# A mixture-of-experts router: the four experts from one Max of eight and a replacement, its tokens a part sooner, its steps dealt denser

## The chip, the cores and the metric

The kernel runs on one core of one Trainium2 chip. A core has five engines with a queue each, taken in order: TensorE (PE in the profile, its weight loads PEld), VectorE (DVE), ScalarE (ACT), GpSimd (POOL) and SyncE (SP, which only starts transfers here). They meet through semaphores. The metric is the device time of one execution in microseconds (us).

## The reference

A transformer block on x of 4 x 512 tokens with 512 features: layer norm, cross attention of 16 heads against a context of 1601 rows (257 image rows and 1344 text rows, a softmax for each kind), a residual sum, layer norm again, and a feed-forward part with a shared network and 32 routed experts. All is float32. What bears on the change is the router, over all 2048 tokens (T), and what the experts do with it:

```python
scores = jax.nn.sigmoid(x @ router_w.T)                     # T x 32
sc = scores + e_bias[None, :]
gs = sc.reshape(T, NG, E // NG)                             # 8 groups of 4 experts
group_scores = lax.top_k(gs, 2)[0].sum(-1)
_, gidx = lax.top_k(group_scores, TKG)                      # 3 groups stay
...
masked = jnp.where(smask > 0, sc, 0.0)
_, topk_idx = lax.top_k(masked, K)                          # 4 experts
topk_w = jnp.take_along_axis(scores, topk_idx, axis=1)
topk_w = topk_w / (topk_w.sum(-1, keepdims=True) + 1e-20) * SCALE
```

Each expert takes the first C = 80 tokens that chose it, in the order of the tokens. Its output for them, silu(x W_gate) * (x W_up) W_down, is scaled by the weight and added to the token's row, beside the shared network's output and the residual.

## The kernel before

The kernel is one long program whose order is written by hand; nothing reschedules it. It goes over the four batches b. For each it makes keys and values of the context (sixteen key parts: four blocks of context by four chunks of features), then the attention, four heads at a time, over 13 key tiles; the output projection, the second layer norm and the router product of batch b (`residual`) run inside the next batch's key parts, and for the last batch inside the tail.

**Routing** (`routing`, called with a batch) returns two lists of small steps for its 512 tokens, laid out as 128 partitions by four token groups (t) by 32 experts. The first list, `work`: the sigmoid on ScalarE (or exponential, sum and reciprocal), the bias, the best two of each group by pairs of maxima and minima, the groups' ranks by comparing all pairs, the mask of the three best groups (`cand`), and then a loop over the four experts that takes for each the maximum, marks where it is, breaks ties to the lowest index by means of `rev` (32, 31, ... 1), adds the mark to `chosen` and pushes the candidate down by 3e38. Then the weights, their DMA into `xw_d` (rows of normed x followed by the 32 weights), and `ranks`: TensorE transposes `chosen` to experts by tokens (four 128x128 transposes, L614), and VectorE makes keys of it in which an earlier token is larger. The second list, `search`: ten Max operations and nine MatchReplace over 80 + 512 keys, which keep each expert's first 80 tokens (`best`) over all batches so far.

The lists of batches 0 and 1 are mixed into the attention loop (two steps a key tile in the last chunk of heads, then seven steps a key part of the next batch). Those of batches 2 and 3 come in the **tail**, `first` and `second`. There the shared network is cut into 32 parts (`units[0]`: gate, up and down products of 8 matmul passes, about 3.43 us each on TensorE), numbered i. A small dealer, `deal(i)`, runs after each part: it spends an account, `SHARE` for each part gone by, 0.3 for a small step and 0.8 for a step of the search, and takes from `first`, then from `second`. `second` is made at part `ready` = 16, since the last batch's router products end with part 15; there `deal(16)` is called ahead of the part itself.

Two parts before the last the kernel empties both lists, and `tokens()` turns `best` into token numbers: two VectorE operations (`past`), a transpose on TensorE (L930), a copy to integers (`tok`). Then six gathers (GpSimd's indirect DMAs, L1003) fetch the tokens of the first six experts out of `xw_d`. The experts follow, one after the other: transposes of the gathered rows (`turn`), `gate_up`, `down`, and a scatter that adds into the output. Their weights, 1.5 MB each, are fetched up to six experts ahead on SyncE's queue, the first of them during the tail's parts (one expert each fourth part).

Of the kernel before, what the change touches and what calls it, by code (L numbers as in the profile page):

```python
# [9 lines left out]
F32 = mybir.dt.float32  # L10
# [3 lines left out]
ALU = mybir.AluOpType  # L14
AX = mybir.AxisListType
# [3 lines left out]
P = 128  # L19
# [7 lines left out]
NQ = L // P  # L27
T = B * L
NT = T // P
E, I, TOPK, NG, TKG = 32, 256, 4, 8, 3  # L30
# [5 lines left out]
BIG = 3.0e38  # L36
# [73 lines left out]
def body(ctx, tc, a, ident, mhalf, logits, x1_d, xw_d, xnT_d, den_d, rec_d, out):  # L110

    nc = tc.nc
# [12 lines left out]
    def psum(dt=F32):  # L125

        shape = [P, 512] if dt is F32 else [P, NQ, P]
        banks.append(banks.pop(0))
        return ring.tile(shape, dt, name="ps", tag=f"bank{banks[-1]}")
# [364 lines left out]

    rt = pool("rt", 1)
    e_b = rt.tile([P, E], F32, name="e_b")
    rev = rt.tile([P, 1, E], F32, name="rev")
    below = rt.tile([P, NG, NG], F32, name="below")

    merged = rt.tile([E, CAP + L], F32, name="merged")  # L500
# [1 line left out]

    def routing_constants():
        nc.scalar.dma_start(e_b, a["e_bias"].partition_broadcast(P))
        nc.gpsimd.iota(rev[:, 0, :], [[-1, E]], base=E, channel_multiplier=0, allow_small_or_imprecise_dtypes=True)
        nc.gpsimd.memset(below, 1.0)

        nc.gpsimd.affine_select(below, below, [[1, NG], [-1, NG]], ALU.is_gt, 0.0, base=0, channel_multiplier=0)
        nc.vector.memset(best, 0.0)

    def routing(b, space, by_exp=False):


        tt, ts, tr = nc.vector.tensor_tensor, nc.vector.tensor_scalar, nc.vector.tensor_reduce
        lo = b * NQ
        taken = []

        def carve(*shape):

            n = NQ  # L520
            for d in shape:
                n *= d
            at = sum(taken)
            taken.append(n)
            names = " ".join("abc"[:len(shape)])
            return space[:, at:at + n].rearrange(
                f"p (t {names}) -> p t {names}", t=NQ, **dict(zip("abc", shape))
            )

        lg = logits[:, lo:lo + NQ, :]  # L530

        both = carve(4 * E)
        first_half, second_half = space[:, :2 * NQ * E], space[:, 2 * NQ * E:4 * NQ * E]
        gt, eq = (x.rearrange("p (t a b) -> p t a b", t=NQ, a=NG) for x in (first_half, second_half))
        cand, hit, sel, chosen = (
            space[:, k * NQ * E:(k + 1) * NQ * E].rearrange("p (t e) -> p t e", t=NQ) for k in range(4)
        )
        sc, sb = carve(E), carve(E)
        m = [carve(NG) for _ in range(4)]
        gs, rank, top = carve(NG), carve(NG), carve(1)  # L540
        g = sb.rearrange("p t (g k) -> p t g k", k=EG)
        one = gs.unsqueeze(3).to_broadcast([P, NQ, NG, NG])
        oth = gs.unsqueeze(2).to_broadcast([P, NQ, NG, NG])
        rv = rev.to_broadcast([P, NQ, E])
        before = below.unsqueeze(1).to_broadcast([P, NQ, NG, NG])

        def wide_(x):
            return x.to_broadcast([P, NQ, E])

        if by_exp:  # L550

            work = [
                lambda: nc.scalar.activation(sc, lg, AF.Exp, scale=-1.0),
                lambda: ts(sc, sc, 1.0, None, ALU.add),
                lambda: nc.vector.reciprocal(sc, sc),
            ]
        else:
            work = [lambda: nc.scalar.activation(sc, lg, AF.Sigmoid)]
        work += [
            lambda: tt(sb, sc, e_b.unsqueeze(1).to_broadcast([P, NQ, E]), ALU.add),  # L560

            lambda: tt(m[0], g[:, :, :, 0], g[:, :, :, 1], ALU.max),
            lambda: tt(m[1], g[:, :, :, 0], g[:, :, :, 1], ALU.min),
            lambda: tt(m[2], g[:, :, :, 2], g[:, :, :, 3], ALU.max),
            lambda: tt(m[3], g[:, :, :, 2], g[:, :, :, 3], ALU.min),
            lambda: tt(m[1], m[1], m[3], ALU.max),
            lambda: tt(m[3], m[0], m[2], ALU.min),
            lambda: tt(m[0], m[0], m[2], ALU.max),
            lambda: tt(m[1], m[1], m[3], ALU.max),
            lambda: tt(gs, m[0], m[1], ALU.add),  # L570

            lambda: tt(gt, oth, one, ALU.is_gt),
            lambda: tt(eq, oth, one, ALU.is_equal),
            lambda: tt(eq, eq, before, ALU.mult),
            lambda: tt(gt, gt, eq, ALU.add),
            lambda: tr(rank, gt, AX.X, ALU.add),
            lambda: ts(rank, rank, float(TKG), None, ALU.is_lt),
            lambda: tt(
                cand.rearrange("p t (g k) -> p t g k", k=EG), g, rank.unsqueeze(3).to_broadcast([P, NQ, NG, EG]), ALU.mult
            ),  # L580
        ]

        for k in range(TOPK):
            into = sel if k else chosen
            work += [
                lambda: tr(top[:, :, 0], cand, AX.X, ALU.max),
                lambda: tt(hit, cand, wide_(top), ALU.is_equal),
                lambda: tt(hit, hit, rv, ALU.mult),
                lambda: tr(top[:, :, 0], hit, AX.X, ALU.max),
                lambda into=into: tt(into, hit, wide_(top), ALU.is_equal),  # L590
            ]
            if k:
                work.append(lambda: tt(chosen, chosen, sel, ALU.add))
            if k < TOPK - 1:
                work.append(
                    lambda into=into: nc.vector.scalar_tensor_tensor(cand, into, -BIG, cand, ALU.mult, ALU.add)
                )
        work += [
            lambda: tt(sb, chosen, sc, ALU.mult),
            lambda: tr(top[:, :, 0], sb, AX.X, ALU.add),  # L600
            lambda: ts(top, top, 1e-20, None, ALU.add),
            lambda: nc.vector.reciprocal(top, top),
            lambda: ts(top, top, SCALE_ROUTE, None, ALU.mult),
            lambda: tt(sb, sb, wide_(top), ALU.mult),
            lambda: nc.sync.dma_start(
                xw_d[lo * P:(lo + NQ) * P, D:].rearrange("(t p) e -> p t e", p=P), sb
            ),
        ]
        key = merged[:, CAP:]

        def ranks():
            ps = psum()
            for i in range(NQ):
                nc.tensor.transpose(ps[:E, i * P:(i + 1) * P], chosen[:, i, :], ident)  # L614
            nc.vector.scalar_tensor_tensor(key, ps[:E, :], float(T), key, ALU.mult, ALU.add)

        work += [
            lambda: nc.gpsimd.iota(
                key, [[-1, L]], base=T - b * L, channel_multiplier=0, allow_small_or_imprecise_dtypes=True
            ),  # L620
            lambda: nc.vector.tensor_copy(merged[:, :CAP], best),
            ranks,
        ]
        search = []
        for j in range(CAP // 8):
            at = best[:, 8 * j:8 * j + 8]
            search.append(lambda at=at: nc.vector.max(at, merged))
            if j < CAP // 8 - 1:
                search.append(lambda at=at: nc.vector.match_replace(merged, at, merged, 0.0))
        return work, search  # L630
# [5 lines left out]
    qT, sq_q, turn, work = queries(0, first_x, L)  # L636
# [281 lines left out]
            nc.sync.dma_start(t, a[name][e])  # L918
            weights.setdefault(e, []).append(t)

    SHARE = 2.4
    AHEAD, WEIGHTS = 6, 6

    def tokens():

        past = ew.tile([E, CAP], F32, name="past", bufs=1)
        nc.vector.tensor_scalar(past, best, T + 0.5, float(T), ALU.is_gt, ALU.mult)
        nc.vector.scalar_tensor_tensor(past, past, float(T), best, ALU.add, ALU.subtract)
        ps = psum()
        nc.tensor.transpose(ps[:CAP, :E], past, ident[:E, :E])  # L930
        nc.vector.tensor_copy(tok, ps[:CAP, :E])
# [149 lines left out]
    for i, u in enumerate(units):  # L1081
        if i < 2:
            continue
        if i == len(units) - 2:
            for f in first + second:
                f()
            first, second = [], []
            tokens()
            for e in range(AHEAD):
                gather(e)  # L1090
        if i == ready:

            space = mid.tile([P, 2, L], F32, name="rb")
            second = sum(routing(B - 1, space.rearrange("p k t -> p (k t)")), [])
            deal(i)
        u()
        for f in side.get(i, ()):
            f()
        later.step()
        deal(i)  # L1100
        if i % 4 == 0 and i // 4 - 1 < WEIGHTS:
            expert_weights(i // 4 - 1)
# [57 lines left out]
```

## Time and profile before

| | |
|---|---|
| three runs | 1705.07, 1705.36, 1710.23 us; median 1705.36 |
| profiled execution | 1705.17 us, its span 1703.5 |
| TensorE | 1681.4 us busy, mean granted clock 0.998 |
| VectorE | 974.6 us busy, 2016 instructions |
| tail: shared parts of units[0] | from about 1327 to 1461 us |
| tail: experts and what is left of the shared network | about 1461 to 1695 us |
| VectorE busy, 1340 to 1400 | 44.6 of 60 us |
| VectorE busy, 1400 to 1460 | 37.9 of 60 us |
| VectorE busy, 1500 to 1600 | 12.9 of 100 us |

Times inside the profile count from the span's start, and a line number (L614) is one of the kernel before. A timeline line gives start, duration, engine, line, operation, what it writes and reads, how many instructions it merges, and in brackets the time that the engine stood idle before it and what it waited for. A matmul's end is modelled, so two consecutive ones overlap a little in the listing; the distance between starts is the better measure. A row of windows gives, for a stretch, its length, then for each engine the busy time and the number of instructions, then the granted clock of TensorE (1.00 is full), the busy share of the DMA engines and GB/s.

### The profile page before, as it was taken

Reading aid. Unit: us, or ns where it says so; the run is one execution under the profiler, and the core shown is the slowest. Engines: PE = TensorE matmul, PEld = TensorE weight load, DVE = VectorE, ACT = ScalarE, POOL = GpSimd, SP = SyncE. Lnnn points to the kernel's source line nnn. Section 1 sums busy time; section 2 is a strip of 40 time slices with the busy share of each in tenths; the row PEclk is TensorE's granted clock in tenths of the full one; section 3 lists DMA queues with packets and bytes.
Section 4 is the critical chain, followed back from the end, with each engine's and each line's share of the span. In section 5 each row is a group of like instructions: output and inputs, shape, how many; then the busy total and the mean of one; then the engine's idle time right before and its main releaser. Section 6 shows DMA issues by size and latency. Waiting matters only on the chain. (4 is left out here: it accounts for less than half of the span.)

```text
span 1703.5 us, 29448 instructions
## 1 busy us (share of the span) xinstructions
PE 1681.4 (99%) x11753; PEld 881.8 (52%) x11753; DVE 974.6 (57%) x2016; ACT 647.3 (38%) x1378; POOL 874.1 (51%) x622
## 2 busy tenths in 40 slices
PE   8999999999999999999999999999999999999997
PEld 4564444456544444565444445654443354677773
DVE  4765555757655549776665597766656767111110
ACT  2135456611354565114545651145557310111111
POOL 3237977332569764426698543276884210233332
PEclk9999999999999999999999999999999999999999
DMA  7000100321100103120000040210002365699964
GB/s 233 1 2 1 27 27 2 114 67 62 38 1 28 27 2 129 51 79 22 2 26 27 2 165 21 75 44 2 14 15 84 112 212 187 199 291 290 296 162 62
DMA packets 67817, 136.30 MB, mean 80 GB/s; under 512 B 16096, under 2 KB 28512, under 8 KB 65632
## 3 DMA queue, kind: packets, MB, share of 16 engines
q1 hardware_dynamic: 60400, 119.91, 21.1%
q0 software_dynamic: 6272, 12.92, 4.1%
q8 instruction: 93, 1.52, 0.4%
q10 hardware_dynamic: 1008, 1.59, 0.3%
q14 instruction: 44, 0.36, 0.1%
HBM read 111.58 MB, written 22.81 MB: 79 GB/s over the span
## 5 line engine op out<-in xcount | busy, mean ns | idle before, releaser
L372 ACT ACTIVATE pT<-ps 128x512 f32<-128x512 f32 (+1 forms) x832 | 429.5, 604 | 346.2 <-PE ps L371 335.7
L334 DVE TENSOR_REDUCE mx<-ps 128x1 f32<-128x512 f32 (+1 forms) x576 | 330.9, 616 | 265.3 <-PE ps L320 265.3
L387 POOL TENSOR_TENSOR acc<-acc,pT 128x1024 f32<-128x1024 f32 x192 | 445.6, 2357 | 3.0 <-ACT pT L372 2.6
L379 PE MATMUL po<-pT,v 128*32 128x512 f32 (+2 forms) x1792 | 222.3, 603 | 0.0
L290 PEld LDWEIGHTS ps<-v_w,cT 128*128 128x128 f32 (+1 forms) x1408 | 169.0, 186 | 102.2 <-DVE mx L334 56.1
L371 PE MATMUL ps<-qT,kT 32*128 32x512 f32 (+1 forms) x1664 | 213.8, 587 | 0.0
L320 PE MATMUL ps<-kT,qT 32*128 32x512 f32 (+1 forms) x1536 | 206.4, 549 | 0.0
L290 PE MATMUL ps<-v_w,cT 128*128 128x128 f32 (+1 forms) x1408 | 197.7, 285 | 0.0
L231 PE MATMUL ps<-cT,wk 128*128 128x512 f32 (+1 forms) x384 | 156.3, 552 | 6.1 <-DMA wk<-in_k_w 6.1
L308 DVE TENSOR_REDUCE mx<-ps 128x1 f32<-128x512 f32 (+2 forms) x256 | 128.1, 562 | 6.4 <-PE ps L305 6.4
L1038 POOL DMA_INDIRECT out<-y,tok x32 | 45.4, 1420 | 133.7 <-DMA out<-y,tok 72.8
L231 PEld LDWEIGHTS ps<-cT,wk 128*128 128x128 f32 x384 | 70.5, 193 | 77.6 <-issue 56.9
L368 PEld LDWEIGHTS <-pick 32*128 32x128 bf16 (+1 forms) x832 | 21.7, 92 | 165.7 <-issue 164.0
L238 POOL TENSOR_TENSOR sq_k<-sq_k,sq 128x512 f32<-128x512 f32 (+2 forms) x48 | 49.5, 1031 | 108.3 <-ACT sq L235 108.0
L298 ACT COPY v<-ps 128x128 f32<-128x128 f32 (+1 forms) x208 | 60.1, 289 | 117.7 <-PE ps L290 117.3
L1028 DVE TENSOR_TENSOR ehT<-ehT,ps 128x160 f32<-128x160 f32 x32 | 10.3, 321 | 158.3 <-ACT ehT L1027 139.1
L394 POOL TENSOR_TENSOR acc<-pT 128x1024 f32<-128x1024 f32 x24 | 56.1, 2359 | 86.9 <-ACT pT L372 54.3
L387 POOL TENSOR_TENSOR pT<-pT 65x1024 f32<-65x1024 f32 x24 | 56.0, 2350 | 87.1 <-PE po L379 78.2
L320 PEld LDWEIGHTS ps<-kT,qT 32*128 32x128 f32 x1536 | 82.1, 183 | 31.0 <-issue 10.1
L387 DVE TENSOR_TENSOR acc<-acc,pT 128x1024 f32<-128x1024 f32 (+1 forms) x72 | 96.7, 1390 | 2.1 <-ACT pT L372 2.1
L379 PEld LDWEIGHTS po<-pT,v 128*32 128x32 f32 (+2 forms) x1792 | 35.0, 107 | 118.6 <-issue 109.3
L368 PE MATMUL ps<-mT,pick 32*128 32x512 bf16 (+1 forms) x832 | 82.6, 386 | 2.4 <-ACT mT L359 2.4
(243 smaller groups left out, 2189.4 us busy)
## 6 DMA issues: line engine op xcount, KB each, us to landing
W_gate<-in_W_gate SPq DMA_DIRECT2D x32, 512.0 KB
W_up<-in_W_up SPq DMA_DIRECT2D x32, 512.0 KB
W_down<-in_W_down SPq DMA_DIRECT2D x32, 512.0 KB
rb<-rec_d SPq DMA_DIRECT2D x64, 128.0 KB
xt<-in_x SPq DMA_DIRECT2D x30, 256.0 KB
cT<-in_ctxT SPq DMA_DIRECT2D x7, 1024.0 KB
wki<-in_k_img_w SPq DMA_DIRECT2D x4, 1024.0 KB
wo<-in_o_w SPq DMA_DIRECT2D x4, 1024.0 KB
```

The lines of the kernel that those rows point to most:

```text
L231: nc.tensor.matmul(ps[:, :n], lhsT=wt[:, k, c * P:(c + 1) * P], rhs=xT[:, k, to], start=k == 0, stop=k == NC - 1)
L290: nc.tensor.matmul(ps[lo:hi, :], lhsT=cTs[bl][:, k, at:at + hi - lo], rhs=ws[bl == NB - 1][:, k, c * P:(c + 1) * P], start=k == 0, stop=k ...
L298: nc.scalar.copy(v[:n, t, :], ps[:n])
L308: nc.vector.tensor_reduce(mx[:, qt, g, bl:bl + 1], ps[:, :n], AX.X, ALU.max, negate=True)
L320: nc.tensor.matmul(ps[:, j * n:(j + 1) * n], lhsT=qT[r:r + HD, c, q * P:(q + 1) * P], rhs=kT[r:r + HD, c, k0:k0 + n], start=True, stop=True,)
L334: nc.vector.tensor_reduce(mx[:, qt, g, i:i + 1], ps[:, :m], AX.X, ALU.max, negate=True)
L368: nc.tensor.matmul(ps[:n], lhsT=pick[r:r + HD, kind(t), :n], rhs=mT[r:r + HD, :], start=True, stop=False)
L371: nc.tensor.matmul(ps[:n], lhsT=kT[r:r + HD, c, t * P:t * P + n], rhs=qT[r:r + HD, c, :], start=False, stop=True)
L372: nc.scalar.activation(pT[:n, g, :], ps[:n], AF.Exp)
L379: nc.tensor.matmul(po[r:r + HD, :], lhsT=v[rows, t, r:r + HD], rhs=pT[rows, g, :], start=start, stop=stop)
L387: (nc.vector if idle else nc.gpsimd).tensor_tensor(to[rows, h, :], to[rows, h, :], pT[rows, h, :], ALU.add)
L394: (nc.vector if idle else nc.gpsimd).tensor_tensor(acc[:, h, :], pTs[0][:, h, :], pTs[1][:, h, :], ALU.add)
```

## The change

Three edits go together.

**The selection.** The loop over four experts and the constant `rev` go. In their place: `cand` becomes the first 32 columns of rows of 36 (`filled`), whose last four hold −1.5e38; for each of the four token groups one Max gives the eight largest of the 32; the last four of these are overwritten by −1.5e38; for each group one MatchReplace writes −3e38 over the first place that holds each of those eight values, so that the four largest are struck out of the candidates, and the other four values find the filling; `chosen` is where the candidate is greater than what is left.

**The tokens.** `tokens` is split: the two VectorE operations (`kept_tokens`) and the emptying of the lists come three parts before the end instead of two; the transpose, the copy and the gathers stay where they were.

**The dealing.** `SHARE` goes from 2.4 to 2.7.

```diff
-        cand, hit, sel, chosen = (
-            space[:, k * NQ * E:(k + 1) * NQ * E].rearrange("p (t e) -> p t e", t=NQ) for k in range(4)
+
+        row_ = E + 8 - TOPK
+        filled, rest_ = (
+            space[:, k * NQ * row_:(k + 1) * NQ * row_].rearrange("p (t e) -> p t e", t=NQ) for k in range(2)
         )
+        cand = filled[:, :, :E]
+        chosen = space[:, 2 * NQ * row_:2 * NQ * row_ + NQ * E].rearrange("p (t e) -> p t e", t=NQ)
...
+            lambda: nc.vector.memset(filled[:, :, E:], -BIG / 2),
             lambda: tt(
                 cand.rearrange("p t (g k) -> p t g k", k=EG), g, rank.unsqueeze(3).to_broadcast([P, NQ, NG, EG]), ALU.mult
             ),
         ]
-        for k in range(TOPK):
-            into = sel if k else chosen
-            work += [
-                lambda: tr(top[:, :, 0], cand, AX.X, ALU.max),
-                lambda: tt(hit, cand, wide_(top), ALU.is_equal),
-                lambda: tt(hit, hit, rv, ALU.mult),
-                lambda: tr(top[:, :, 0], hit, AX.X, ALU.max),
-                lambda into=into: tt(into, hit, wide_(top), ALU.is_equal),
-            ]
-            if k:
-                work.append(lambda: tt(chosen, chosen, sel, ALU.add))
-            if k < TOPK - 1:
-                work.append(
-                    lambda into=into: nc.vector.scalar_tensor_tensor(cand, into, -BIG, cand, ALU.mult, ALU.add)
-                )
+        work += [lambda t=t: nc.vector.max(largest8[:, t, :], cand[:, t, :]) for t in range(NQ)]
+        work += [lambda: nc.vector.memset(largest8[:, :, TOPK:], -BIG / 2)]
+        work += [
+            lambda t=t: nc.vector.match_replace(rest_[:, t, :], largest8[:, t, :], filled[:, t, :], -BIG)
+            for t in range(NQ)
+        ]
+        work += [lambda: tt(chosen, cand, rest_[:, :, :E], ALU.is_gt)]
...
-    SHARE = 2.4
+    SHARE = 2.7
...
-    def tokens():
+    def kept_tokens():
         past = ew.tile([E, CAP], F32, name="past", bufs=1)
         nc.vector.tensor_scalar(past, best, T + 0.5, float(T), ALU.is_gt, ALU.mult)
         nc.vector.scalar_tensor_tensor(past, past, float(T), best, ALU.add, ALU.subtract)
+        return past
+
+    def tokens(past):
         ps = psum()
...
-        if i == len(units) - 2:
+        if i == len(units) - 3:
             for f in first + second:
                 f()
             first, second = [], []
-            tokens()
+            past = kept_tokens()
+        if i == len(units) - 2:
+            tokens(past)
             for e in range(AHEAD):
                 gather(e)
```

More of the change, by code (lines that the diff above doesn't have):

```diff
@@ L496, in body @@
     e_b = rt.tile([P, E], F32, name="e_b")
-    rev = rt.tile([P, 1, E], F32, name="rev")
     below = rt.tile([P, NG, NG], F32, name="below")
@@ L504, in routing_constants @@
         nc.scalar.dma_start(e_b, a["e_bias"].partition_broadcast(P))
-        nc.gpsimd.iota(rev[:, 0, :], [[-1, E]], base=E, channel_multiplier=0, allow_small_or_imprecise_dtypes=True)
         nc.gpsimd.memset(below, 1.0)
@@ L534, in routing @@
         gt, eq = (x.rearrange("p (t a b) -> p t a b", t=NQ, a=NG) for x in (first_half, second_half))
-        cand, hit, sel, chosen = (
-            space[:, k * NQ * E:(k + 1) * NQ * E].rearrange("p (t e) -> p t e", t=NQ) for k in range(4)
-        )
+        row_ = E + 8 - TOPK
+        filled, rest_ = (
+            space[:, k * NQ * row_:(k + 1) * NQ * row_].rearrange("p (t e) -> p t e", t=NQ) for k in range(2)
+        )
+        cand = filled[:, :, :E]
+        chosen = space[:, 2 * NQ * row_:2 * NQ * row_ + NQ * E].rearrange("p (t e) -> p t e", t=NQ)
         sc, sb = carve(E), carve(E)
         m = [carve(NG) for _ in range(4)]
-        gs, rank, top = carve(NG), carve(NG), carve(1)
+        gs, rank, top, largest8 = carve(NG), carve(NG), carve(1), carve(8)
         g = sb.rearrange("p t (g k) -> p t g k", k=EG)
@@ L543, in routing @@
         oth = gs.unsqueeze(2).to_broadcast([P, NQ, NG, NG])
-        rv = rev.to_broadcast([P, NQ, E])
         before = below.unsqueeze(1).to_broadcast([P, NQ, NG, NG])
```

## The prediction

> **What bounds the kernel now.** I read the page's busy table first, then the list of what TensorE waited for over the whole span, then the order of time around the two places that the change moves.
>
> ```profile
> PE 1681.4 (99%) x11753; PEld 881.8 (52%) x11753; DVE 974.6 (57%) x2016; ACT 647.3 (38%) x1378; POOL 874.1 (51%) x622
> ...
> PE ps L231 <- DMA wk<-in_k_w: 6.1, 1, 6.1
> ...
> PE ps L930 <- DVE past L928: 1.2, 1, 1.2
> PE ps L225 <- DVE xpT L1016: 0.7, 1, 0.7
> PE ps L614 <- DVE v L593: 0.7, 2, 0.3
> ```
>
> The first line is the page's, the others are from the list of TensorE's waits (total, times, longest). TensorE is busy 99% of the span and waits 12.9 us in all in that list, 6.1 of them for the first weights. So VectorE time saved is worth nothing by itself: routing can gain only the waits in which TensorE stands for it, L930's 1.2 us (tokens) and L614's 0.7 us (ranks, two of its four executions). **The most this change can gain is 1.9 us, 0.11%.** But any new wait of TensorE is paid in full.
>
> **Fewer VectorE operations.** In the timeline of the last batch's selection, the loop over the four experts (L586 to L596) is 26 operations, each about 0.32 us after the one before: 8.3 us. Its successor is one memset, four Max, one memset, four MatchReplace (each a load of the values and a replacement) and one comparison. The search of the ranks shows both new kinds at another size:
>
> ```profile
> 1427.14 0.77 DVE L627 MAX8 best<-merged 32x8 f32<-32x592 f32 x1
> 1429.74 0.69 DVE L977 TENSOR_TENSOR x1r<-x1r,ps 128x512 f32<-128x512 f32 x1 [1.83 <-DMA x1r<-x_d]
> 1430.35 0.07 DVE L629 MATCH_VALUE_LOAD merged<-best,merged 32x8 f32 x1
> 1430.42 0.75 DVE L629 MATCH_REPLACE8 merged<-best,merged 32x592 f32<-32x592 f32 x1
> ```
>
> Columns are start, duration, operation. A TensorTensor of 512 columns takes 0.69 and one of 128 takes 0.29, about 1.04 ns a column. At that slope, 32 columns cost Max 0.77 − 560 × 0.00104 = 0.19, and 36 cost the replacement 0.17, with 0.07 for its load. The sizes are not in the trace, so these are estimates. Back to back: 4 × 0.19 + 4 × 0.25 + two memsets of about 0.1 + 0.32 = 2.3 us; four such in a row overlap by some 0.1 us where none waits for the one before (L562 to L563 start 0.13 apart with 0.21 each), so at least 1.6; with twice the fixed cost at most 3.2. I take 2.2. Some 6 us of VectorE time go in each of four routings, 24 us in all, hidden behind TensorE now: worth 0.
>
> **Denser dealing, the first of the two last routings.** A list was 54 small steps and 19 of the search, 54 × 0.3 + 19 × 0.8 = 31.4 of the dealer's units; it becomes 39 and 19, 26.9. At 2.7 a part instead of 2.4, the four transposes of ranks come after part 6 (gate 3, at about 1354.2) instead of after part 8 (1361.1). On VectorE the mask step L578 ended at 1350.0, behind GpSimd sums that run to 1351.2; adding 2.2 us for the new search and 0.69 for the hT product queued in it gives 1352.9, and 1354.2 if the memset and the mask both wait for GpSimd. TensorE needs it at 1354.2: cost 0, up to 0.3. SyncE now issues the 64 KB of weights (L605) ahead of the next x tile, which so starts at about 1355 instead of 1348.0; x is wanted by the sum at 1368.6, hidden. Ahead of it stand the first expert's weights, behind it the second's, first used after 1460.
>
> **Denser dealing, the last routing: the step that decides.** It may begin at part 16 (`ready`), with whatever the dealer's account allows by then. Before: 15 × 2.4 − 31.4 = 4.6, so 16 steps, and the trace has just these (sigmoid and L560 to L576) before it goes on with the shared network's products. After: 15 × 2.7 − 26.9 = 13.6. All 39 steps cost 11.7, so **all 39, with the transposes of ranks, and three search steps are issued in one burst before part 16**. The changed program's order has it so: on TensorE the four transposes stand directly behind the last router product (L225, rw) and ahead of gate 2, where before they stood six parts later. TensorE takes its queue in order, so gate 2 and everything behind it wait for the whole selection, which cannot begin before that same router product:
>
> ```profile
> 1403.56 0.97 PE L225 MATMUL ps<-rw,xnT 128*128 128x32 f32 x8
> 1404.37 3.68 PE L225 MATMUL ps<-xT,shared_gate 128*128 128x512 f32 x8
> ...
> 1404.57 0.19 DVE L476 COPY logits<-ps 128x32 f32<-128x32 f32 x1
> 1405.13 0.29 DVE L560 TENSOR_TENSOR rb<-rb,e_b 128x128 f32<-128x128 f32 x1 [0.38 <-ACT rb L558]
> ...
> 1408.80 0.42 DVE L576 TENSOR_REDUCE rb<-rb 128x32 f32<-128x256 f32 x1
> ```
>
> Up to the rank sums it is measured: 1409.25. Then the comparison (0.21), the memset (0.1) and the mask (0.32): 1409.9. Then Max, memset, replacement and comparison, some 1.9 without the first memset: 1411.8, and 0.1 to TensorE: 1411.9 against 1404.4. **Gap 7.5 us**, at least 6.8, at most 8.5. The transposes' own 0.45 us only move. Nothing can fill the gap: all parts stand behind it. ScalarE's Silu and VectorE's hT product wait for it too.
>
> **The clock behind that gap.** TensorE has no gap over 1.4 us between its first and last matmul now, so what follows such a gap is seen only at the two ends:
>
> ```profile
> 1694.00:1697.00 3.00, 0.46 (x2) 0.00 (x0) 0.00 (x0) 0.58 (x1) 0.85 (x1) 1.00 0.66 70
> 1697.00:1703.00 6.00, 0.00 (x0) 0.00 (x0) 0.00 (x0) 0.00 (x0) 0.00 (x0) 0.51 0.23 39
> ...
> 8.00 0.34 PEld L231 LDWEIGHTS ps<-cT,wk 128*128 128x128 f32 x1 [0.52 <-issue]
> ...
> 11.60 0.19 PEld L231 LDWEIGHTS ps<-cT,wk 128*128 128x128 f32 x1 [0.24 <-issue]
> ```
>
> In the windows, the third number from the end is the granted clock: TensorE's last matmul ends at 1694.5, and the clock is at half by about 1697. In the loads after the first wait, from 6.13 to 11.17, the six passes are 0.85 apart instead of 0.43, so 2.5 us were lost although the clock column has 1.00 there. The Trainium skill (TensorE: Matmul & The Clock Gate, the goals table "Why this matters for your kernels", and Part 1) speaks against the change: no idle gaps over some 3 us, since one idle window halves the clock and about 3.4 us of work must pass before it is full again. By the rule the loss is 1.7 us; by the row 2.5. I take 2.3; with no loss at all the low end.
>
> **Tokens one part sooner.** The two VectorE steps that make `past` run before up 2 (the search has ended by part 22), so the transpose goes at once: −1.2. The copy into `tok` now stands behind up 2's hT product (0.69), ending about 0.6 us sooner than before; the first six gathers start that much sooner, while TensorE reaches the first expert's transposes 1.2 sooner. Landing takes 3.2 us in the trace, the second gather lands about a microsecond ahead: hidden. If it weren't, half of the 1.2 is lost.
>
> **The routings inside the attention loop.** Sixteen key parts take seven steps each; ranks come two parts sooner, behind the q norms' transposes at 686.9. The selection there ends by about 683.5: L614's two waits go, −0.7 (0 if VectorE's backlog of sums is longer). The weights' DMA goes ahead of that of the reciprocals by about a microsecond; the sum that needs those starts at 699.1 now. Late in the last routing, the same DMA stands ahead of xT and of the weights of experts 3 and 4 in SyncE's queue, about 9 us later than now; TensorE is later by as much, xT is used 13 us after its issue now, those experts start after 1480: 0. The dropped iota is off the path.
>
> **The sum**, against the profiled execution (1705.17; span 1703.5 and 1.7 outside it; the runs' median is 1705.36, 0.2 above): 7.5 + 2.3 − 1.2 − 0.7 = +7.9, **1713.1**.
>
> **Rivals.**
> - *Full clock.* The gap does not halve the clock: 7.5 − 1.9 = +5.6, 1710.8. For it: the clock column at the start shows no drop. Against: the passes there, and the tail.
> - *Longer selection.* The small new operations cost 0.5 each (the gap is 9.7) and 6 us of work pass before the clock is back: 9.7 + 3.0 − 1.2 = +11.5, 1716.7. For it: VectorE steps that meet GpSimd take 1.3 instead of 0.3. Against: GpSimd is idle from 1403 to 1455.
> - *Absorbed, not slower.* The experts' stage from 1480 to 1600 is paced by their weights (DMA busy 0.95 to 0.97 there), and a TensorE that comes late finds more of them loaded and catches up: −1.9, 1703.3. It decides if TensorE has idle time there to give back. Against: two loads and a down projection make 5.5 us an expert, the pitch seen, and no weight is in the list of waits.
> - *The burst is not there* (the dealer's account is not as I add it): 1703.3 too, against the program's order.
>
> **Chances.** Forecast 0.77, full clock 0.10, longer 0.09, the last two 0.04. No change means within 0.3%, 5.1 us, what a measurement of this kernel can tell: 1700.2 to 1710.5. Full clock straddles 1710.5; half of it counts as same, and a little of the forecast's low end. Slower 0.89, same 0.10, faster 0.01. The range: 6.8 − 1.9 gives 1710.1, 8.5 + 2.6 − 1.2 + 0.3 gives 1715.4; I take 1709.9 to 1715.6.
>
> **What would show it.** One TensorE wait of 7 to 8.5 us at the transposes of ranks for the comparison that makes `chosen`; granted clock under 1 in the slice behind it and passes 0.86 apart for 3 to 5 us; L930's wait gone; VectorE some 24 us less busy. Wrong if TensorE shows no wait over 2 us there, or if the experts' stage shortens.

## The result, and the profile after

The changed kernel takes 1712.69 us (median of 8 runs, 1711.63 to 1716.63), the kernel before, run beside it, 1707.38 (8 runs, 1705.07 to 1710.23): **a ratio of 1.004, 95% interval 1.0031 to 1.005**. The profiled execution took 1712.04 us against 1705.17 (+6.9), its span 1710.3 against 1703.5 (+6.8). The ratios here and below are the recorded ones, with their intervals; the quotients of the medians differ from them by up to 0.0009 (here 1.0031).

The head of the changed kernel's page, and its row of busy times:

```profile
span 1710.3 us, 29407 instructions
...
PE 1683.6 (98%) x11753; PEld 882.6 (52%) x11753; DVE 950.5 (56%) x1972; ACT 647.3 (38%) x1378; POOL 873.7 (51%) x621
```

VectorE has 44 instructions and 24.1 us less to do, and the kernel is slower. The list of what TensorE waited for (total, times, longest) says where:

```profile
PE ps L609 <- DVE rb L592: 7.0, 1, 7.0
PE ps L231 <- DMA wk<-in_k_w: 5.9, 1, 5.9
PE ps L368 <- ACT mT L359: 2.4, 4, 0.6
PE ps L468 <- DVE xn L220: 1.8, 3, 0.6
PE ps L225 <- DVE xpT L1015: 0.7, 1, 0.7
```

The waits for the tokens (L930) and for the ranks inside the attention loop (L614) are gone. One new wait of 7.0 us heads the list: the ranks' transposes, now L609, for the comparison at L592 that makes `chosen`. In TensorE's timeline it stands between the last router product and gate 2:

```profile
1402.88 0.97 PE L225 MATMUL ps<-rw,xnT 128*128 128x32 f32 x8
1410.90 1.04 PE L609 MATMUL ps<-ident,rb 128*32 128x128 f32 x4 [7.05 <-DVE rb L592]
1411.73 5.12 PE L225 MATMUL ps<-xT,shared_gate 128*128 128x512 f32 x8
1416.69 3.60 PE L225 MATMUL ps<-xT,shared_up 128*128 128x512 f32 x8
```

Gate 2 takes 4.96 us from its start to that of up 2; a gate at full clock takes 3.43 to 3.44. Windows of the same stretch (the third number from the end is the granted clock):

```profile
1404.00:1407.00 3.00, 0.00 (x0) 0.00 (x0) 2.42 (x13) 1.59 (x2) 0.00 (x0) 1.00 0.23 87
1407.00:1411.00 4.00, 0.10 (x1) 0.10 (x2) 3.64 (x22) 0.00 (x0) 0.00 (x0) 0.62 0.00 0
1411.00:1414.00 3.00, 3.00 (x7) 1.55 (x8) 2.76 (x10) 0.00 (x0) 0.00 (x0) 0.50 0.16 27
1414.00:1415.00 1.00, 1.00 (x3) 0.36 (x2) 0.97 (x3) 0.00 (x0) 0.00 (x0) 0.60 0.47 137
1415.00:1418.00 3.00, 3.00 (x9) 1.33 (x8) 0.60 (x1) 0.60 (x1) 0.00 (x0) 1.00 0.96 300
```

TensorE is idle, VectorE is busy with small steps, and the clock falls to half at about 1408 (0.62 is the mean of 1407 to 1411) and is full again at about 1414.8 (0.60 is the mean of 1414 to 1415), 3.9 us after work resumed. What VectorE does at the end of the gap, in its timeline:

```profile
1408.70 0.07 DVE L579 MEMSET rb<- 128x16 f32 x1
1408.79 0.29 DVE L580 TENSOR_TENSOR rb<-rb 128x128 f32<-128x128 f32 x1
1409.12 0.47 DVE L586 MAX8 rb<-rb 128x8 f32<-128x32 f32 x4
1409.66 0.07 DVE L587 MEMSET rb<- 128x16 f32 x1
1409.77 0.09 DVE L589 MATCH_VALUE_LOAD rb<-rb 128x8 f32 x1
1409.85 0.18 DVE L589 MATCH_REPLACE8 rb<-rb 128x36 f32<-128x36 f32 x1
...
1410.56 0.29 DVE L592 TENSOR_TENSOR rb<-rb 128x128 f32<-128x128 f32 x1
```

From the first Max to the end of the comparison it is 1.73 us: the selection itself is as cheap as hoped.

**The 6.8 us, taken apart.** I subtracted the starts of the same matmuls before and after, and followed how far the changed kernel is behind (in us):

| matmul | before | after | behind |
|---|---|---|---|
| first product of the shared network's tail | 1326.81 | 1326.14 | −0.7 |
| up 2, behind the gap | 1407.88 | 1416.69 | +8.8 |
| the part behind the old place of the transposes (part 22, down) | 1425.48 | 1433.86 | +8.4 |
| gate of part 30, behind the tokens | 1454.48 | 1461.57 | +7.1 |
| first expert's transposes | 1461.45 | 1468.54 | +7.1 |
| the shared network's last down products, behind the experts | 1666.83 | 1673.93 | +7.1 |

The gap from 1403.69, where part 16 would have started, to 1410.90 is 7.2; the clock costs 1.9 (0.4 in the transposes, 1.5 in gate 2); the transposes only moved; the tokens give back 1.3, and the changed kernel entered the tail 0.7 early: 7.2 + 1.9 − 1.3 − 0.7 = +7.1. The experts' stage has the same length in both, 205.4 us. In the span, 0.3 of this is missing. It goes behind the last row, where the eleven profiles differ among themselves anyway (36.2 to 36.7 us to the end).

The 0.7 ahead of the tail is the sum of two things, as the first products of the program show, before and then after:

```profile
6.13 9.49 PE L231 MATMUL ps<-cT,wk 128*128 128x512 f32 x16 [6.13 <-DMA wk<-in_k_w]
5.87 10.12 PE L231 MATMUL ps<-cT,wk 128*128 128x512 f32 x16 [5.87 <-DMA wk<-in_k_w]
```

They end at 15.6 before and at 16.0 after, though the program is the same up to there. So the changed kernel's execution began 0.4 late, and the attention loop gave back 1.0: some 0.4 at each of the two places of L614, and 0.3 at one weight load (L320, at 1147.6), which waited for ScalarE before and does not after. Counted from the end of these first products, the tail begins after 1311.1 to 1311.3 us in the three profiles with the old selection and after 1310.1 to 1310.2 in the eight with the new one. Below, "from the first products" means counted in this way.

### The profile page after: what moved, and what is told of

Read it like the earlier page. It is cut to its first block, busy times and chain, and to the rows that moved or that the text cites. A ratio compares the mean times of both kernels' runs of the same rounds, so it can differ in the third digit from the quotient of the medians.

```text
span 1710.3 us, 29407 instructions
## 1 busy us (share of the span) xinstructions
PE 1683.6 (98%) x11753; PEld 882.6 (52%) x11753; DVE 950.5 (56%) x1972; ACT 647.3 (38%) x1378; POOL 873.7 (51%) x621
## 5 line engine op out<-in xcount | busy, mean ns | idle before, releaser
L320 PE MATMUL ps<-kT,qT 32*128 32x512 f32 (+1 forms) x1536 | 206.1, 549 | 0.0
L320 PEld LDWEIGHTS ps<-kT,qT 32*128 32x128 f32 x1536 | 82.0, 183 | 30.8 <-issue 10.1
```

Of the source, the lines that this page charges most:

```text
L320: nc.tensor.matmul(ps[:, j * n:(j + 1) * n], lhsT=qT[r:r + HD, c, q * P:(q + 1) * P], rhs=kT[r:r + HD, c, k0:k0 + n], start=True, stop=True,)
```

## The experiments

The theory: inside the changed kernel it is the denser dealing that makes the loss, because it puts all 39 steps of the last routing, TensorE's transposes among them, ahead of part 16; the gap costs its length, and some 2 us more by the slow clock behind it. The rivals: the new operations or the moved tokens cost something themselves; the clock behind the gap costs nothing; the whole loss comes elsewhere. Each ratio below is to the kernel before, run again on the same chip (medians 1706.1 to 1706.3).

**The change without the denser dealing.**

```diff
-    SHARE = 2.7
+    SHARE = 2.4
```

> The changed kernel with SHARE back at 2.4: the account at part 16 is 15 x 2.4 - 26.9 = 9.1, so 31 of the 39 steps (chosen included) go ahead of part 16 and the transposes of ranks come behind part 17. My theory (the burst with its transposes is the whole loss): no TensorE wait over 1 us at L609, granted clock 1.00 throughout, L930's wait still gone; 1.9 us under the kernel before, so a ratio of 0.998 to 1.000. Rival (the new small Max and MatchReplace steps, or something else in the new selection, slow the kernel wherever they stand): still 5 us or more above the kernel before, ratio 1.003 or more.

Measured: 1702.63 (12 runs), **ratio 0.9988 (0.9978 to 0.9998)**. TensorE's timeline:

```profile
1402.28 3.68 PE L225 MATMUL ps<-xT,shared_gate 128*128 128x512 f32 x8
1405.80 3.60 PE L225 MATMUL ps<-xT,shared_up 128*128 128x512 f32 x8
1409.59 0.60 PE L609 MATMUL ps<-ident,rb 128*32 128x128 f32 x4 [0.20 <-DVE rb L592]
```

The transposes come behind gate 2 and up 2, and of the 7.0 us of wait 0.2 are left. In the changed kernel, then, the loss is the dealing's. What remains of the change gains about the 1.9 us that the prediction called its most (0.11%): from the first products, 1.0 us ahead of the tail and 0.9 in it. The gain is near what can be told from nothing (the interval allows 0.3 to 3.8 us), but this version beats both kernels.

**The dealing without the new selection** (the kernel before, 2.7).

```diff
-    SHARE = 2.4
+    SHARE = 2.7
```

> The kernel before with SHARE 2.7 alone (old selection, old tokens). The account at part 16 is 15 x 2.7 - 31.4 = 9.1, so 31 of the old 54 steps, no ranks in the burst. My theory (what counts is where the transposes of ranks stand against the time VectorE has the choice ready): in batch 2's routing they come after part 7, at 1357.6, while VectorE, busy without a pause there, has the choice at 1360.8: a wait of about 3.2 us; in batch 3's they come after part 19 and VectorE is about 1.2 us late. Together 4.4 us over the kernel before, 5.5 if the clock halves behind the longer one: ratio 1.0026 to 1.0033. Rival (dealing denser is harmless by itself, only its meeting with the short lists at part 16 hurts): no wait over 1 us, ratio 1.000.

Measured: 1708.85 (20 runs), ratio 1.001 (1.0003 to 1.0017). From TensorE's timeline:

```profile
1359.51 0.61 PE L614 MATMUL ps<-ident,space 128*32 128x128 f32 x4 [1.21 <-DVE space L593]
```

The direction is that of the theory, the size a miss: one new wait of 1.2 us in the first of the two last routings and 0.1 in the last. I had put VectorE too late: `chosen` was ready at about 1359.45, not at 1360.8. The old selection's 54 steps are more than the account allows at part 16, so the transposes stay behind products there. Neither the dealing nor the selection makes the gap alone; a shorter list and a larger allowance do it together.

**The old list in one burst** (the kernel before).

```diff
+            spent -= 11.7
             deal(i)
```

> The kernel before with its account lowered by 11.7 at part 16, so that all 54 old steps of the last routing, its transposes included, and one search step go in one burst ahead of that part. My theory (the burst costs the length of VectorE's chain, plus the halved clock): old loop of 26 steps x 0.325 = 8.4 us instead of 1.5, so the choice is ready at 1418.2, the wait is 13.7 us, 1.9 more for the clock: 15.6 us over the kernel before, ratio 1.0092. Rival (Max and MatchReplace on short rows make the gap of the changed kernel): a gap of 7 us or less, ratio 1.005 or less.

Measured: 1722.65 (4 runs), **ratio 1.0099 (1.008 to 1.0118)**:

```profile
1417.74 1.04 PE L614 MATMUL ps<-ident,rb 128*32 128x128 f32 x4 [13.46 <-DVE rb L593]
1418.57 6.10 PE L225 MATMUL ps<-xT,shared_gate 128*128 128x512 f32 x8
1424.50 3.60 PE L225 MATMUL ps<-xT,shared_up 128*128 128x512 f32 x8
```

With the four-expert loop the same place costs 13.5 us instead of 7.0. The place of the transposes is what costs, and Max and MatchReplace shorten it by 6.4 us.

**The gap filled with matmuls** (the changed kernel; it adds seven products that nobody reads, so its time holds added work).

```diff
+            ps = psum()
+            for k in range(7):
+                nc.tensor.matmul(ps, lhsT=sg[:, 0, :P], rhs=su[:, k % NC, :], start=True, stop=True)
             deal(i)
```

> The changed kernel with seven matmuls of 128x512 ahead of the last routing's transposes, on a PSUM bank that nobody reads: about 6.0 us of TensorE work inside the gap of 7.2. My theory (the gap's length is set by VectorE and the halved clock is paid on top): the wait falls to about 1 us, the granted clock stays at 1.00, the transposes start at the same time as in the changed kernel, and the kernel is 1.9 us faster than the changed one: about 5 us above the kernel before, ratio 1.0028. Rival (the halved clock costs nothing because what comes behind has slack): same time as the changed kernel, ratio 1.004.

Measured: 1710.53 (14 runs), ratio 1.0022 (1.0014 to 1.003):

```profile
1402.19 6.25 PE L1098 MATMUL ps<-shared_up,shared_gate 128*128 128x512 f32 x14
1409.41 0.61 PE L609 MATMUL ps<-ident,rb 128*32 128x128 f32 x4 [0.96 <-DVE rb L592]
1409.86 3.60 PE L225 MATMUL ps<-xT,shared_gate 128*128 128x512 f32 x8
1413.30 3.60 PE L225 MATMUL ps<-xT,shared_up 128*128 128x512 f32 x8
```

The transposes stand 7.22 us behind the place where the gap began, as in the changed kernel (7.21); but the clock stays full, and from the transposes to up 2 it is 3.89 us instead of 5.79. **With useless work in the gap TensorE is 1.9 us sooner at up 2 than with nothing in it**: the clock's part of this execution, measured alone. In whole times the ratio falls from 1.004 to 1.0022; 1.9 us would be 0.0011, and the intervals leave room for that and for more.

**One product in the gap** (the changed kernel; the same burst, only the transposes behind part 16).

```diff
-            deal(i)
+            while len(second) > 2 * CAP // 8:
+                spent += 0.3
+                second.pop(0)()
```

> The changed kernel with the same burst at part 16, except that its last step, the transposes of ranks, goes behind part 16 instead of ahead of it. VectorE's chain is untouched. My theory: one part of 3.43 us fills the gap, the wait is 7.05 - 3.4 = 3.6 us; with the clock still full in a gap this short the kernel is 1.8 us above the one before (ratio 1.001), with the clock halved some 3.8 us (1.0022). Rival (the burst on VectorE is the loss, by the products of hT that wait behind it, not the transposes' place): as slow as the changed kernel, 1.004.

Measured: 1709.94 (9 runs), ratio 1.0016 (1.0006 to 1.0027):

```profile
1409.88 1.04 PE L609 MATMUL ps<-ident,rb 128*32 128x128 f32 x4 [3.54 <-DVE rb L592]
1410.71 4.56 PE L225 MATMUL ps<-xT,shared_up 128*128 128x512 f32 x8
```

One gate (3.4 us) takes its length off the gap, which is 3.54 instead of 7.05. The clock falls in this gap too: the transposes are 0.83 ahead of the next start, as after the long gap, and up 2 takes 4.39 us to the next start (1415.10) instead of 3.43. About 1.35 us are lost to the clock.

**A share between the two.**

```diff
-    SHARE = 2.7
+    SHARE = 2.55
```

> The changed kernel with SHARE 2.55, the nearest round value below the cliff that I compute: 15 x 2.55 - 26.9 = 11.35, less than the 11.7 that 39 steps cost by one step, so all but the ranks go ahead of part 16 and the transposes behind part 17. My theory: like SHARE 2.4, 1.9 us under the kernel before (ratio 0.998 to 1.000), no wait at L609. Rival (denser dealing costs in proportion, by crowding VectorE): about half of the loss of 2.7 remains, ratio 1.001 to 1.003.

Measured: 1706.45 (12 runs), ratio 1.0 (0.9991 to 1.0009), at the upper end of what I expected. The transposes wait 0.2 as with 2.4. But a wait that I had not foreseen stands where the first was removed. From SyncE's timeline (start, duration of the issue, line, operation):

```profile
1411.38 0.38 SPq L600 DMA_DIRECT2D xw_d<-rb  x1
1411.85 0.58 SPq L941 DMA_DIRECT2D xT<-xnT_d  x1
```

and from TensorE's:

```profile
1419.51 5.35 PE L225 MATMUL ps<-xT,shared_gate 128*128 128x512 f32 x8 [2.13 <-DMA xT<-xnT_d]
1424.70 3.60 PE L225 MATMUL ps<-xT,shared_up 128*128 128x512 f32 x8
```

The burst of 38 steps holds the DMA of the routing weights (L600) too, and SyncE, which takes its queue in order, now waits for the weights before it issues xT. xT arrives 2.1 us after TensorE wants it. That is not all: the gate behind this wait takes 5.19 us instead of 3.43, so another 1.8 us go. The windows there:

```profile
1419.00:1420.00 1.00, 0.49 (x1) 0.50 (x2) 0.97 (x3) 0.00 (x0) 0.00 (x0) 0.74 1.03 422
1422.00:1423.00 1.00, 1.00 (x3) 0.36 (x2) 0.97 (x3) 0.00 (x0) 0.00 (x0) 0.55 1.02 414
```

The clock, full until then, halves at about 1419.5 and is full again at about 1422.9. A wait of 2.1 us has cost 3.9.

**The same share, the burst cut ahead of that DMA.** Of the 38 steps 31 are issued; the rest come behind part 17, where the queue has xT already.

```diff
-            deal(i)
+            while len(second) > 27:
+                second.pop(0)()
+            spent = (i - 1) * SHARE
```

> The changed kernel with SHARE 2.55 and the burst at part 16 cut after 31 steps: the transposes of ranks stand where they stand in the plain SHARE 2.55 run, behind part 17, but the DMA of the routing weights now comes behind part 16's fetch of xT in SyncE's queue instead of ahead of it. My theory (what SHARE 2.55 loses against 2.4 is the 2.1 us wait for xT, and that comes from the queue): xT is issued at about 1403 instead of 1412, no wait for it, ratio 0.998 to 0.9995. Rival (the denser dealing itself, or the experts' gathers, cost it): still 1.000.

Measured: 1703.96 (21 runs), ratio 0.999 (0.9983 to 0.9997):

```profile
1403.80 0.58 SPq L941 DMA_DIRECT2D xT<-xnT_d  x1
...
1412.51 0.38 SPq L600 DMA_DIRECT2D xw_d<-rb  x1
```

xT is issued 8 us sooner, its wait is gone, and so is the loss against the share of 2.4: from the first products, the first expert begins after 1443.8 us here, after 1443.9 with the share of 2.4 and after 1447.9 with the plain 2.55. The order in SyncE's queue was the cause.

**The tokens back at their old place** (share 2.4).

```diff
-        if i == len(units) - 3:
+        if i == len(units) - 2:
...
-            past = kept_tokens()
-        if i == len(units) - 2:
-            tokens(past)
+            tokens(kept_tokens())
```

> The new selection with SHARE 2.4 (the run before with the ratio 0.9988) and the two VectorE steps of the tokens back where they were, two parts before the end. My theory (the split of tokens is worth the wait it removes): the transpose of past waits for VectorE again, 1.2 us, and the ratio rises from 0.9988 to 0.9995. Rival (the wait is only moved, to the expert's first rows): ratio stays at 0.9988 and the wait comes back elsewhere.

Measured: 1705.5 (22 runs), ratio 0.9994 (0.9987 to 1.0001), against 0.9988 with the tokens moved. The intervals overlap, so the times alone don't settle 1.2 us; the trace does. The list of waits has the line

```profile
PE ps L929 <- DVE past L923: 1.2, 1, 1.2
```

which is absent where the tokens are moved, and from the first products the first expert begins after 1445.2 us instead of 1443.9.

**The changed kernel again.**

> The changed kernel itself, on the same chip as these: a wait of 7.0 us at L609, the granted clock at half behind it, ratio 1.004 as before. If the loss came from something that differs between chips or executions, the ratio would leave 1.003 to 1.005.

Measured: 1713.77 (4 runs), ratio 1.0049 (1.003 to 1.0068):

```profile
1409.91 1.03 PE L609 MATMUL ps<-ident,rb 128*32 128x128 f32 x4 [7.05 <-DVE rb L592]
1410.74 4.58 PE L225 MATMUL ps<-xT,shared_gate 128*128 128x512 f32 x8
1415.16 3.60 PE L225 MATMUL ps<-xT,shared_up 128*128 128x512 f32 x8
```

The gap is the same to 0.01 us, and the clock halves again. But from the transposes to up 2 it is 5.25 us, not 5.79: with 3.89 at full clock, the clock costs 1.4 us in this execution and 1.9 in the first. The program does not fix this term.

## Why the prediction was right, point by point

The prediction of 1713.1 stood for +7.9 us over the profiled execution; the profiles give +6.9 and the ratio 1.004 gives 6.8. That the median, 1712.69, is only 0.4 from the forecast is partly luck: the kernel before came out at 1707.38, 2.0 above the median of its first three runs. The mechanism is the one that was forecast; three of its four terms were 0.3 to 0.9 us off. By its steps:

- **What can be gained, at most 1.9 us:** right to 0.1. Without the dealing the change gains 2.0 us, by the ratio (0.9988 of 1706) and by the profiles (1.0 and 0.9).
- **VectorE's 24 us are worth nothing:** 24.1 us are gone, and no stage is shorter for them. Only in the burst do they count, where VectorE is what TensorE waits for (13.5 against 7.0).
- **The burst ahead of part 16:** right, the transposes stand directly behind the last router product.
- **The gap, 7.5:** 7.2. Most of the difference is in the new operations, put at 1.9 and measured at 1.73: four Max were put at 4 × 0.19 less 0.1 and take 0.47 in all, so they overlap more than estimated; MatchReplace with its load was put at 0.25 and follows the one before after 0.17.
- **The clock, 2.3:** 1.9 in one execution and 1.4 in the other, to either side of the 1.7 estimated from the Trainium skill (TensorE: Matmul & The Clock Gate, Part 1); I had leaned to the 2.5 of the row at the start of the span. The page's 3.4 us of work until full clock were 3.9 and 2.8 here. With the gap filled the loss is gone, which is what makes it the clock's. The limit of "some 3 us" for a gap, which the prediction took from the same page, is too long here: 2.13 us were enough with the share of 2.55.
- **The tokens, −1.2:** −1.3 in the starts of the matmuls, and the gathers stay hidden: the first expert has no wait.
- **The attention loop, −0.7:** −1.0. The −0.7 in the starts agrees by luck, since this execution began 0.4 late. The term left out the short wait at L320, and each place of L614 gave 0.4, not 0.35.
- **The first of the two last routings, 0:** no wait there.
- **xT 9 us later, 0:** it comes 8 us later and costs nothing in this kernel, by one of the two reasons given: TensorE is late by as much. With a share of 2.55, which has no gap, the same order costs 2.1 us of wait and 1.8 of clock. So the other reason, that xT was used 13 us after its issue, would not have covered it.

The rivals: *full clock* falls with the windows and with the filled gap. What spoke for it, the 1.00 of the clock column at the start, was no reading: the clock's record in that trace begins only at 10.9 us. *Longer selection* falls with 0.47 us for four Max. *Absorbed* falls with the experts' stage of 205.4 us in both profiles. *No burst* falls with the order of TensorE's rows.

## What to carry to other kernels

A dealer that counts steps by their cost on one engine must also ask what they put into the in-order queues of the others: one waiting transpose in TensorE's queue, or one waiting store in SyncE's, holds up everything issued behind it. Making steps cheaper can itself cause this, since more of them fit into one allowance. Cut a burst ahead of its first step on another engine, leave work between, and price a TensorE gap of some 2 us or more with the slow clock after it.

## What the hardware did that I had not expected

**The gap need not be long.** In the kernel with one product in the gap, windows around it:

```profile
1406.00:1409.00 3.00, 0.34 (x1) 0.00 (x0) 2.71 (x16) 0.60 (x1) 0.00 (x0) 1.00 0.00 0
1409.00:1410.00 1.00, 0.12 (x1) 0.12 (x2) 0.93 (x9) 0.00 (x0) 0.00 (x0) 0.61 0.00 0
1410.00:1412.00 2.00, 2.00 (x6) 1.19 (x6) 1.83 (x8) 0.00 (x0) 0.00 (x0) 0.50 0.00 0
1412.00:1413.00 1.00, 1.00 (x3) 0.35 (x2) 0.93 (x3) 0.00 (x0) 0.00 (x0) 0.68 0.41 66
```

A gap of 3.54 us still halves the clock, 2.9 us after the last matmul. From such windows, in which a mean of 0.61 says that the clock fell at 1409.2, all five gaps between matmuls that halved the clock (us; the last from a mean of 0.76 in 1406 to 1407 and of 0.71 in 1423 to 1424):

| kernel | gap | last matmul to half clock | time at half clock | work resumed to full clock | lost |
|---|---|---|---|---|---|
| share 2.55, wait for xT | 2.1 | 2.1 | 3.4 | 3.4 | 1.8 |
| one product in the gap | 3.5 | 2.9 | 3.4 | 2.7 | 1.35 |
| changed kernel | 7.0 | 4.1 | 6.8 | 3.9 | 1.9 |
| changed kernel again | 7.0 | 3.0 | 6.8 | 2.8 | 1.4 |
| old list in one burst | 13.5 | 2.2 | 17.1 | 5.8 | 2.9 |

The windows of the changed kernel again, for comparison with the first:

```profile
1405.00:1406.00 1.00, 0.00 (x0) 0.00 (x0) 0.93 (x5) 0.00 (x0) 0.00 (x0) 0.94 0.00 0
1412.00:1413.00 1.00, 1.00 (x2) 0.33 (x1) 0.93 (x3) 0.00 (x0) 0.00 (x0) 0.64 0.41 66
```

The loss is about half the time from the resumption to the full clock, as half speed implies. That time varies from 2.7 to 5.8 us and does not follow from the gap alone: two executions of one program have 3.9 and 2.8. What is regular is the time at half clock: 3.4, 3.4, 6.8, 6.8 and 17.1 us are 1, 1, 2, 2 and 5 times 3.41. So in these traces the clock changes as if it were set only every 3.41 us, at moments that the program does not choose, and the loss depends on where a gap falls between them. Waits of TensorE in the tail of 1.6 us and less (1.2 for `past`, 1.5 and 1.6 for gathers) left the clock full in every profile. A single wait of 2.1 us halved it, just as work resumed; whether each of that length would is not shown.

**Executions differ before the change begins.** The first products of the program, at half pace at first (passes 0.85 us apart instead of 0.43), end between 14.6 and 16.2 us in the eleven profiles. From there to the first place of the change, at 687, all eleven keep their distance from each other to 0.1 us. A single pair of profiles can so differ by 1.6 us for a reason that is not the change's.

**The experts' stage varies too.** It took 205.4 us in seven of the eleven profiles, but 206.4 with share 2.55, 207.0 with the filled gap, 209.4 with one product in the gap and 209.0 with the tokens put back, each with TensorE waits for the experts' gathers (0.8 to 3.0 us). Runs of one kernel spread over some 6 us (1701.95 to 1708.16 with share 2.4). Whether these gather waits belong to a kernel's order or to an execution was not settled. They limit the fine comparisons above. For the kernel with one product in the gap, 3.5 of gap and 1.35 of clock less 1.9 give 1.0017, inside the interval of its runs (1.0006 to 1.0027); with the 4.0 us by which its experts' stage was longer it would be 1.0041, outside. So its gather waits seem to belong to the profiled execution; that is argued, not shown.
